# Layer 0's mixture of experts, from all experts inside the recurrence to picked experts behind it

## The chip, the cores and the metric

The kernel runs on one core of a Trainium2 chip. A core has five engines with their own instruction queues: PE (matrix products; its weight loads stand as PEld), DVE (vector), ACT (activation functions), POOL (general, here also the issuer of gathers and scatters) and SP (issues the plain transfers). [...] The metric is the time of one execution in microseconds (us), as the device reports it.

## What is computed

Four layers work on x (4 batches, 512 tokens, 256 numbers). Each adds an attention part and a feed-forward part, both behind a layer norm and a gate. Layer 0's attention part is an LSTM over the 512 tokens with an attention in each step, so its steps depend on each other. Its feed-forward part, which the change moves, is a mixture of 8 experts of which each token uses one:

```python
x = x + tanh(g_xattn[0]) * L0_xattn(ctx, layernorm(x), ...)        # LSTM, 512 steps
x = x + tanh(g_ffn[0])   * L0_ffn(layernorm(x), w1, b1, w2, b2, wr, br)

def L0_ffn(x, w1, b1, w2, b2, wr, br):            # x: 2048 tokens of 256
    probs = softmax(x @ wr + br)                  # 8 experts
    top_p, top_i = top_k(probs, 2)
    gate, top1 = top_p[:, 0] / (top_p[:, 0] + top_p[:, 1]), top_i[:, 0]
    for e in range(8):                            # w1[e]: 256 x 1024, w2[e]: 1024 x 256
        hout = gelu(x @ w1[e] + b1[e]) @ w2[e] + b2[e]
        out += where(top1 == e, hout * gate, 0)
```

Layer 1 has a cross attention of x with the context in both directions, and 8 gated experts of which two are used; layer 2 an additive attention and 8 experts with those kept that hold 0.8 of the probability; layer 3 a 16-head attention and a quantised product.

## The kernel before, in words

**Recurrence.** `lstm` loads the weights, and `recurrence` runs over 512 steps (`lstm_step`). A step is a chain that goes from engine to engine: products with the hidden state (PE), a transposition (DVE, L821), tanh (ACT, L832 and L837), scores (PE, L844), softmax (DVE and ACT, L855 to L864), products with the attention's weights (PE, L868), gates (DVE L877, ACT L880), cell and hidden state (L886 to L897). L897, on DVE, writes the new hidden state and ends the step.

Other work is put in the gaps of the steps by a planner, `Later`. It holds tasks in queues by engine and kind (`soon`, `chain`, `bulk`, `down`), with what they wait for and a cost, and `later.fill(engine, budget)` writes the next ready ones at fixed places of the step: on PE after the scores (`SLOT_B` tasks) and after the attention's products (`SLOT_C`), on ACT, DVE, POOL and SP at one place each. After the last step `later.drain()` writes all that is left.

After each 64 steps `block_tasks` adds the tasks of that block of 64 tokens by 4 batches (256 tokens): load x (L513), the cell's gates (L529, L541), cell and hidden state (L552 to L565), add to x (L590). Then come layer norm, router and, for each of the 8 experts on all 256 tokens, 32 instructions of products up (L720), gelu (L730), 32 down (L751) and the weighted sum into x (L758). Weights of 1 MB come through `net.fetch` into a ring of three places for `up` and three for `down` (L122, L125). At the end the block goes back into `xtok` (L799), which holds x for all tokens. ACT's Exp and Tanh share a function table, while gelu and Sqrt each need another: the step reloads its own at L895.

`net.fill` copies x into DRAM scratch, 2 MB at a time, once each 8 steps (L94), so that no unset row is read later.

**Tail.** Behind the recurrence layers 1 and 2 use picked experts alone. `picks_of` sorts one batch: layer norm, router (`ranked`), weights, the place of each pick (`g_to`), and indirect DMAs on POOL that scatter the rows by expert into DRAM (L1227). A group is two batches. `Blocks` computes a group in blocks of one expert: `load` reads the expert's number and its rows' place into registers on SP and loads rows and weights (L1293) into the same ring, `turn` transposes the rows, `work_1` or `work_2` does the products (L1392 to L1431 are its activations), `out` stores the result. `sure` computes the first `kind.sure` blocks, and `rest` enters a branch if the group has more (L1457), which computes `kind.step` blocks, all through one ring place. `back` gathers the results by indirect DMAs (L1481) and adds them to `xtok` (L1473, DVE).

PE's instructions keep the order in which the program writes them (`Ordered`), so `weave(main, side, ratio)` sets it: after each step of `main`, `ratio` steps of `side`. The order of the tail before: layer 1's context, attention of batch 0, attention of batch 1 together with batch 0's sort, batch 1's sort, then layer 1's first group beside batches 2 and 3, and so on through the layers. The products of all of the tail stand under the helper's line, L940.

Of the kernel before, what the change touches and what calls it, by code (L numbers as in the profile page):

```python
# [21 lines left out]
FP = mybir.dt.float32  # L22
# [7 lines left out]
P = 128  # L30
# [4 lines left out]
TPB = S // P  # L35
# [5 lines left out]
SLOT_B, SLOT_C = 2, 2  # L41
# [4 lines left out]
class Net:  # L46


    def __init__(self, ctx, tc, a):
# [26 lines left out]
        self.at = {"up": 0, "down": 0}  # L76
        self.ready = {part: deque() for part in ("up", "down")}
        self.coming = {part: deque() for part in ("up", "down")}
        for part in self.coming.values():
            part.extend((0, e) for _ in range(NBLK) for e in range(NE))  # L80
# [29 lines left out]

    def fetch(self, part=None):

        nc, a = self.nc, self.a
        for part in (part,) if part else ("up", "down"):
            if not self.coming[part]:
                continue
            layer, e = self.coming[part].popleft()
            i = self.at[part] % 3
            self.at[part] += 1
            if part == "down":  # L120
                w = self.ring[:, i, 1].rearrange("p (f d) -> p f d", d=D)
                nc.sync.dma_start(w, a[f"L{layer}_w2"][e])  # L122
            else:
                w = self.ring[:, i, 0].rearrange("p (k f) -> p k f", k=KD)
                nc.sync.dma_start(w, a[f"L{layer}_w1"][e])  # L125
            self.ready[part].append((layer, e, w))

    def take(self, part, layer, e):
        got = self.ready[part].popleft()
        assert got[:2] == (layer, e)  # L130
        return got[2]
# [113 lines left out]
def lstm(net):  # L245
    tc, nc, a = net.tc, net.nc, net.a
    with ExitStack() as st:
# [19 lines left out]
        with tc.tile_pool(name="l_set", bufs=1) as pool, tc.tile_pool(  # L267
# [22 lines left out]
            net.fetch()  # L290
            net.fetch()
# [64 lines left out]
            down=st.enter_context(tc.tile_pool(name="l_down", bufs=2, space=PSUM)),  # L356
        )
# [3 lines left out]
def recurrence(net, w, pools):  # L361
# [3 lines left out]
    moe0 = load_moe0(net, one)  # L365
# [18 lines left out]
    for t in range(S):  # L384
        i, u = divmod(t, P)
        if u == 0 and i + 1 < TPB:
            norm_x(net, later, w, pools, xb, i + 1)
        v = t % TB
        if v == 0:
            n = t // TB  # L390

            assert n < 3 or all(x["at"] for x in used[n - 3])
            hb = two.tile([P, 2, TB, NB], FP, name="hb", bufs=3)
            cb = two.tile([P, 2, TB, NB], FP, name="cb", bufs=3)
        if t % 32 == 0 and t and t // 32 + 1 < NJ:
            gates_of_block(net, later, w, pools, xb, ge, t // 32 + 1)
        lstm_step(net, pools["step"], ps, w, later, ge, t, h, hb[:, :, v], cb[:, :, v], ga[t % 2], ga[1 - t % 2])
        h = hb[:, :, v]
        if t > TB and t % 8 == 4:
            net.fill()  # L400
        if v == TB - 1:
            used.append(block_tasks(net, later, w, moe0, pools, n, hb, cb))
# [77 lines left out]
def load_moe0(net, pool):  # L480
    nc, a = net.nc, net.a
    m = {}
    m["wr"] = pool.tile([P, KD, NE], FP, name="m0_wr")
    nc.sync.dma_start(m["wr"], a["L0_wr"])
    m["br"] = pool.tile([P, NE], FP, name="m0_br")
    nc.sync.dma_start(m["br"], a["L0_br"].partition_broadcast(P))
    m["b1"] = pool.tile([P, NE, 8], FP, name="m0_b1")
    nc.sync.dma_start(m["b1"], a["L0_b1"])
    m["b2"] = pool.tile([NE, D], FP, name="m0_b2")
    nc.sync.dma_start(m["b2"], a["L0_b2"])  # L490
    return m


def block_tasks(net, later, w, m, pools, n, hb, cb):
# [5 lines left out]
    one, two, up, down = pools["one"], pools["two"], pools["up"], pools["down"]  # L500
    box = {}
    add = later.add

# [73 lines left out]
    sums = []  # L577
    for p in range(2):
# [16 lines left out]
        def total(p=p):  # L595
            if p == 0:
                box["st"] = two.tile([P, 2, 6], FP, name="st")
                box["mv"] = two.tile([P, 2, 2], FP, name="mv2")
            yield nc.vector.bn_stats(box["st"][:, p, :], box["xh"][:, p, :])
            yield nc.vector.bn_aggr(box["mv"][:, p, :], box["st"][:, p, :])  # L600

        t = chain("PE", turn, hs, takes=["up"], frees=[("g2", acts[0])] if p else [])
        chain("DVE", lambda put=put: put(0), [t, loaded], 0.5)
        p1 = chain("DVE", lambda put=put: put(1), [t, loaded], 0.5, frees=[("up", t)])
        sums.append(chain("DVE", total, [p1], 0.8))

    def root():
        box["rs"] = two.tile([P, 2], FP, name="rs")
        later.table = "sqrt"
        yield nc.scalar.activation(box["rs"], box["mv"][:, :, 1], AF.Sqrt, bias=net.eps)  # L610

    r = chain("ACT", root, sums)
    r = chain("DVE", lambda: [nc.vector.reciprocal(box["rs"], box["rs"])], [r], 0.2)
    outs = []
    for p in range(2):
        cell = {}

        def normal(p=p, cell=cell):
            cell["xn"] = two.tile([P, D], FP, name="xn")
            yield nc.gpsimd.tensor_scalar(  # L620
                cell["xn"], box["xh"][:, p, :], box["mv"][:, p, 0:1], box["rs"][:, p : p + 1],
                ALU.subtract, ALU.mult,
            )

        def turn(cell=cell):
            cell["ps"] = up.tile([P, KD, P], FP, name="ps_xt", tag="up")
            for k in range(KD):
                yield nc.tensor.transpose(cell["ps"][:, k, :], cell["xn"][:, ts(k, P)], net.ident)

        def out(p=p, cell=cell):  # L630
            if p == 0:
                box["x"] = two.tile([P, KD, 256], FP, name="xm")
            yield nc.scalar.copy(box["x"][:, :, ts(p, P)], cell["ps"])

        k = chain("POOL", normal, [r], takes=["xn"])
        t = chain("PE", turn, [k], takes=["up"], frees=[("xn", k)])
        outs.append(chain("ACT", out, [t], cost=0.6, frees=[("up", t)]))


    def logits():  # L640
        box["pr"] = up.tile([P, 2, NE], FP, name="ps_route", tag="up")
        for p in range(2):
            for k in range(KD):
                yield nc.tensor.matmul(
                    box["pr"][:, p, :], lhsT=box["x"][:, k, ts(p, P)], rhs=m["wr"][:, k, :],
                    start=k == 0, stop=k == KD - 1,
                )

    head = last = chain("PE", logits, outs, takes=["up"])

    def tile(name, *shape):
        box[name] = two.tile([P, *shape], FP, name=f"r_{name}")
        return box[name]

    v, N2 = nc.vector, (2, NE)
    steps = [
        lambda: v.tensor_add(tile("lg", *N2), box["pr"], bc(m["br"], 1, 2)),
        lambda: v.tensor_reduce(tile("mx", 2), box["lg"], AX.X, ALU.max),
        lambda: v.tensor_sub(tile("e", *N2), box["lg"], bc(box["mx"], 2, NE)),
        "exp",  # L660
        lambda: v.tensor_tensor(tile("over", *N2, NE), bc(box["e"], 2, NE), bc(box["e"], 3, NE), ALU.is_gt),
        lambda: v.tensor_tensor(tile("same", *N2, NE), bc(box["e"], 2, NE), bc(box["e"], 3, NE), ALU.is_equal),
        lambda: v.tensor_mul(box["same"], box["same"], bc(net.before, 1, 2)),
        lambda: v.tensor_add(box["over"], box["over"], box["same"]),
        lambda: v.tensor_reduce(tile("rank", *N2), box["over"], AX.X, ALU.add),
        lambda: v.scalar_tensor_tensor(tile("two", *N2), box["rank"], 1.5, box["e"], ALU.is_lt, ALU.mult),
        lambda: v.tensor_reduce(tile("den", 2), box["two"], AX.X, ALU.add),
        lambda: v.reciprocal(box["den"], box["den"]),
        lambda: v.scalar_tensor_tensor(box["two"], box["rank"], 0.5, box["e"], ALU.is_lt, ALU.mult),
        lambda: v.tensor_mul(tile("comb", *N2), box["two"], bc(box["den"], 2, NE)),  # L670
        lambda: v.tensor_scalar_mul(box["comb"], box["comb"], net.gate[:, 1, 0:1]),
    ]
    for i, f in enumerate(steps):
        if f == "exp":
            last = chain("ACT", lambda: [nc.scalar.activation(box["e"], box["e"], AF.Exp)], [last], 0.4)
        else:
            last = chain("DVE", lambda f=f: [f()], [last], 0.3, frees=[] if i else [("up", head)])


    def turn():  # L680
        box["pc"] = up.tile([NE, 2, P], FP, name="ps_ct", tag="up")
        for p in range(2):
            yield nc.tensor.transpose(box["pc"][:, p, :], box["comb"][:, p, :], net.ident)

    def out():
        box["cT"] = two.tile([NE, 256], FP, name="cT")
        yield nc.scalar.copy(box["cT"], box["pc"].rearrange("p b t -> p (b t)"))

    comb = last
    t = chain("PE", turn, [comb], takes=["up"])  # L690
# [1496 lines left out]
```

## Time and profile before

| what | value |
| --- | --- |
| median of 10 runs | 5555.59 us (5550.56 to 5563.15) |
| the profiled execution's own time | 5553.95 us |
| its span, first to last instruction | 5552.2 us |
| instructions | 142169 |
| PE, DVE, ACT, POOL busy | 86%, 44%, 48%, 8% of the span |
| first and last L897 (step ends) | 53.4 and 3379.0 us |
| first turn of layer 1's first block | 3823.4 us |
| four branches of `rest` | all not entered |

How to read it: an engine's busy time is the union of its instructions' times, and a product's own time includes its way through a pipeline, so that many of 0.4 us follow each other each 0.22 us. In a group's row, after the count, come busy time, the mean of one in ns, and the engine's idle time just before with what ended it. "DVEq" or "PEldq" is an engine's sequencer. A window's row gives its length, then the busy time of each engine that took part.

### The profile page before, as it was taken

The page shows a single profiled execution, that of the slowest core. Times are in us where ns is not written, and L with a number is a line of the kernel's source. Part 1 is how long each engine was busy: PE and PEld are TensorE (multiplying, and loading weights), DVE is VectorE, ACT ScalarE, POOL GpSimd, SP SyncE. Part 2 cuts the span into 40 slices and gives each one's busy share as a digit, 9 for nine tenths or more (in the row PEclk, how much of TensorE's full clock was granted, in tenths as well). Part 3 has the DMA queues.
Part 4 walks back from the last instruction along what each step waited for, and adds up shares of the span by engine and source line. Part 5 has one row for each costly group of instructions (what it writes and reads, how often), then busy time and mean ns, then how long its engine had stood idle before and what let it go on. Part 6 is the DMA issues. An engine that isn't in the chain of part 4 may idle for free. (4 is left out here: it accounts for less than half of the span.)

```text
span 5552.2 us, 142169 instructions
## 1 busy us (share of the span) xinstructions
PE 4760.0 (86%) x57504; PEld 2662.8 (48%) x57504; DVE 2443.1 (44%) x10804; ACT 2683.0 (48%) x8540; POOL 465.4 (8%) x884
## 2 busy tenths in 40 slices
PE   5667799999999999999999999987988599869967
PEld 2223344444444444444444446864533365757744
DVE  3555555555555555555555552123523332121145
ACT  2344565656665656566666663211266165213212
POOL 1000000100000100100000010001111201130030
PEclk8999999999999999999999999998999799989968
DMA  5000012112212112112212102413644333544210
GB/s 204 2 2 2 10 70 92 63 66 78 85 70 87 63 63 102 55 70 80 77 63 85 56 33 96 140 62 110 197 139 129 135 114 127 180 160 141 93 52 8
DMA packets 117988, 480.66 MB, mean 87 GB/s; under 512 B 23473, under 2 KB 62787, under 8 KB 87939
## 3 DMA queue, kind: packets, MB, share of 16 engines
q1 hardware_dynamic: 105026, 437.85, 22.4%
q0 software_dynamic: 12288, 33.57, 1.8%
q8 instruction: 455, 7.45, 0.6%
q14 instruction: 219, 1.79, 0.1%
HBM read 434.65 MB, written 137.89 MB: 103 GB/s over the span
## 5 line engine op out<-in xcount | busy, mean ns | idle before, releaser
L844 PE MATMUL psr<-e,vrep 128*32 128x64 f32 x16384 | 590.8, 232 | 50.0 <-ACT e L832 47.3
L868 PE MATMUL psf<-fw,alb 128*4 128x256 f32 x8192 | 540.6, 381 | 100.6 <-DVE alb L864 96.0
L844 PEld LDWEIGHTS psr<-e,vrep 128*32 128x32 f32 x16384 | 390.5, 108 | 409.9 <-ACT e L832 287.0
L720 PE MATMUL ps_up<-xm,ring 128*128 128x256 f32 x2048 | 546.9, 398 | 8.7 <-ACT h L730 8.3
L825 PE MATMUL psf<-whh,hb 128*4 128x256 f32 x8176 | 543.0, 383 | 0.7 <-issue 0.7
L751 PE MATMUL ps_down<-ring,h 128*128 128x256 f32 x2048 | 542.4, 396 | 0.0
L832 ACT ACTIVATE e<-fproj,hw 128x64 f32<-128x64 f32 x1024 | 297.9, 337 | 364.0 <-DVE hw L821 363.9
L880 ACT ACTIVATE ga<-gt 128x24 f32<-128x24 f32 (+1 forms) x1024 | 170.4, 214 | 572.5 <-DVE gt L877 571.3
L855 DVE TENSOR_REDUCE stat<-psr 128x1 f32<-128x64 f32 x1024 | 230.2, 225 | 448.5 <-PE psr L844 448.5
L720 PEld LDWEIGHTS ps_up<-xm,ring 128*128 128x128 f32 x2048 | 356.7, 189 | 143.2 <-issue 79.8
L751 PEld LDWEIGHTS ps_down<-ring,h 128*128 128x128 f32 x2048 | 359.1, 189 | 131.2 <-issue 83.3
L856 ACT ACTIVATE al<-psr,stat 128x64 f32<-128x64 f32 x1024 | 320.4, 313 | 183.0 <-DVE stat L855 183.0
L877 DVE STREAM_TRANSPOSE gt<-psf 128x192 f32<-128x192 f32 (+1 forms) x1024 | 263.1, 295 | 321.6 <-PE psf L868 321.1
L816 PE MATMUL psa<-wh,hb 128*4 128x64 f32 x8176 | 209.4, 220 | 203.4 <-DVE hb L897 199.3
L940 PE MATMUL ps_up<-xT,ring 128*128 128x256 f32 x1280 | 309.5, 393 | 72.2 <-ACT h L1429 48.8
L1721 ACT ACTIVATE h<-featT,txtT 128x512 f32<-128x512 f32 x512 | 324.7, 711 | 96.8 <-PE psr L940 62.2
L474 PE MATMUL psf<-ge,ident 128*4 128x256 f32 x4096 | 320.8, 385 | 57.4 <-DVE gt L877 57.3
L836 DVE TENSOR_TENSOR e<-fproj,hw 128x128 f32<-128x128 f32 x1536 | 361.5, 290 | 17.6
L898 POOL COPY cb<-ga 128x8 f32<-128x8 f32 x512 | 96.9, 189 | 3151.7 <-DVE ga L890 3151.7
L837 ACT ACTIVATE e<-e 128x128 f32<-128x128 f32 x1536 | 354.8, 293 | 2.6 <-DVE e L836 2.1
L816 PEld LDWEIGHTS psa<-wh,hb 128*4 128x4 f32 x8176 | 114.4, 86 | 463.5 <-DVE hb L897 463.5
L868 PEld LDWEIGHTS psf<-fw,alb 128*4 128x4 f32 x8192 | 123.1, 84 | 422.9 <-DVE alb L864 413.2
(418 smaller groups left out, 6438.3 us busy)
## 6 DMA issues: line engine op xcount, KB each, us to landing
ring<-in_L_w_dram SPq DMA_DIRECT2D x208, 1024.0 KB
ring<-in_L_w_dram SPq DMA_DIRECT2D x120, 512.0 KB
res<-y SPq DMA_DIRECT2D x120, 128.0 KB
rows_in<-rows SPq DMA_DIRECT2D x40, 256.0 KB
rows_in<-rows SPq DMA_DIRECT2D x40, 128.0 KB
rows<-in_x_dram SPq DMA_DIRECT2D x2, 1920.0 KB
res<-in_x_dram SPq DMA_DIRECT2D x2, 1920.0 KB
xtok<-in_x_dram SPq DMA_DIRECT2D x4, 512.0 KB
```

Of the source, the lines that this page charges most:

```text
L474: net.tc.keep_in_program_order(net.nc.tensor.matmul(out[32 * q : 32 * q + NB, :], lhsT=sel, rhs=ge[t // 32][:, ts(q, 256)], start=True, st ...
L720: yield nc.tensor.matmul(cell["ps"][:, f % 2, :], lhsT=ex["w"][:, k, ts(f, P)], rhs=box["x"][:, k, :], start=k == 0, stop=k == KD - 1,)
L751: yield nc.tensor.matmul(cell["ps"], lhsT=ex["h"][:, f, ts(p, P)], rhs=ex["down"][:, f, :], start=f == 0, stop=f == 7,)
L816: pin(nc.tensor.matmul(ps["a"][32 * q : 32 * q + NB, :], lhsT=h[:, c, :], rhs=w["wh"][:, c, ts(q, 64)], start=c == 0, stop=c == 1,))
L825: pin(nc.tensor.matmul(psf[32 * q : 32 * q + NB, :], lhsT=h[:, c, :], rhs=w["whh"][:, c, ts(q, 256)], start=False, stop=False,))
L836: pin(nc.vector.tensor_add(e[:, p, c], w["fproj"][:, p, c], bc(hw[:, c, ts(p, 2)], 2, SC)))
L837: pin(nc.scalar.activation(e[:, p, c], e[:, p, c], AF.Tanh))
L844: pin(nc.tensor.matmul(ps["r"][p][ts(2 * b + i, 32), :], lhsT=w["vrep"][:, c, :], rhs=ev[:, ::-1, :] if i else ev, start=c == 0, stop=c == ...
L856: pin(nc.scalar.activation(al[:, p], ps["r"][p], AF.Exp, bias=stat[:, p, 0:1], accum_out=stat[:, p, 1:2]))
L868: pin(nc.tensor.matmul(psf[32 * q : 32 * q + NB, :], lhsT=alb[:, p], rhs=w["fw"][:, p, ts(q, 256)], start=False, stop=p == 1,))
L940: return lambda *a, **k: self.tc.keep_in_program_order(fn(*a, **k))
L1721: nc.scalar.activation(h, featT[:, ec, :], AF.Tanh, bias=w["txtT"][:, ec, col : col + 1])
```

## The change

- `block_tasks` ends with the new x of the block, which goes straight to `xtok`. Norm, router, experts and their fetches leave the recurrence, `load_moe0`, `fetch` and `take` with them. `SLOT_B` goes from 2 to 1, and `net.fill` runs each 6 steps, since four more scratch tensors are to be filled.
- Layer 0 becomes a third `Kind`: one pick a token, blocks of 256, 8 sure blocks, 3 in `rest`. `top_1` makes its weights, `second_bias` (out of `top_p`) adds the second bias, `work_2` gets Gelu.
- The tail's order: both sorts of group 0 taken in turns with both contexts; group 0's blocks beside group 1's sorts, `rest`; group 1's blocks beside the gathers of group 0, layer 1's attention of batches 0 and 1 and their sorts, `rest`; then layer 1's first group, with the gathers of group 1 ahead of its side work.

```diff
-SLOT_B, SLOT_C = 2, 2
+SLOT_B, SLOT_C = 1, 2
...
-        if t > TB and t % 8 == 4:
+        if t > TB and t % 6 == 4:
             net.fill()
         if v == TB - 1:
-            used.append(block_tasks(net, later, w, moe0, pools, n, hb, cb))
+            used.append(block_tasks(net, later, w, pools, n, hb, cb))
...
         t = chain("PE", turn, hs, takes=["up"], frees=[("g2", acts[0])] if p else [])
         chain("DVE", lambda put=put: put(0), [t, loaded], 0.5)
-        p1 = chain("DVE", lambda put=put: put(1), [t, loaded], 0.5, frees=[("up", t)])
-        sums.append(chain("DVE", total, [p1], 0.8))
-    def root():
...
+        done = chain("DVE", lambda put=put: put(1), [t, loaded], 0.5, frees=[("up", t)])
...
-    add("SP", store, [last_put], frees=[("block", loaded)])
+    chain("SP", store, [done], frees=[("block", loaded)])
...
-KINDS = {1: Kind(1, 2, 128, 20, 3), 2: Kind(2, 6, 256, 20, 4)}
+KINDS = {0: Kind(0, 1, 256, 8, 3), 1: Kind(1, 2, 128, 20, 3), 2: Kind(2, 6, 256, 20, 4)}
...
+def top_1(t, pool, m, b, rank, key, keep, comb):
+
+    v, net = t.nc.vector, t.net
+    v.scalar_tensor_tensor(comb, rank, 1.5, key, ALU.is_lt, ALU.mult)
+    den = pool.tile([P, TPB], FP, name="g_den")
+    v.tensor_reduce(den, comb, AX.X, ALU.add)
+    v.reciprocal(den, den)
+    v.tensor_scalar_mul(den, den, net.gate[:, 1, 0:1])
+    v.tensor_single_scalar(keep, rank, 0.5, ALU.is_lt)
+    v.tensor_mul(comb, keep, key)
+    v.tensor_mul(comb, comb, bc(den, 2, NE))
+    yield
+    yield from second_bias(t, pool, m, b, comb)
...
-                    if i >= self.on_scalar:
+                    if self.kind.layer == 0:
+                        nc.scalar.activation(h[:, f, :], ps[:, n, :], AF.Gelu, bias=bias)
+                    elif i >= self.on_scalar:
...
-            context_l1(t, w1, p1)
-            pk = Picks(t, sort)
...
-            b1 = Blocks(t, KINDS[1], first, got[1][1], KINDS[1].sure % 3)
-            b0 = Blocks(t, KINDS[1], first, got[1][0], 0, b1)
-            run(behind(1, l1, 0))
-            weave(b0.sure(), chain(behind(1, l1, 2), context_l2(t, w2, p2)), 1.1)
+            def contexts():
+                for _ in range(2):
+                    yield
+                context_l1(t, w1, p1)
+                yield
+                yield from context_l2(t, w2, p2)
...
+            with tc.tile_pool(name="sort_too", bufs=1) as too:
+                run(turns(sorted_by(0, 0), sorted_by(0, 1, {"sort": too}), contexts()))
+            yg = work_1.enter_context(tc.tile_pool(name="first_back", bufs=1))
+
+            def back_0(g):
+                return back(t, yg, KINDS[0], groups[g], groups[g], got[0][g], 4)
+
+            with tc.tile_pool(name="zero", bufs=2) as zero:
+                b0 = Blocks(t, KINDS[1], None, got[1][0], at[2])
+                a1 = Blocks(t, KINDS[0], zero, got[0][1], at[1], b0)
+                a0 = Blocks(t, KINDS[0], zero, got[0][0], at[0], a1)
+                weave(a0.sure(), chain(sorted_by(0, 2), sorted_by(0, 3)), 0.8)
+                a0.rest()
+                weave(a1.sure(), chain(back_0(0), behind(1, l1, 0)), 1.6)
+                a1.rest()
+            first = beside("first", 2)
+            b0.pool, b0.next = first, Blocks(t, KINDS[1], first, got[1][1], at[3])
+            b1 = b0.next
+            weave(b0.sure(), chain(back_0(1), behind(1, l1, 2)), 1.1)
             b0.rest()
```

## The prediction, on record before the changed kernel ran

> **What bounds the kernel now.** I read the page's busy table first (PE 86%), then the step times of the recurrence, then the stretches behind it, then who waits there, because the share of 86% is a mean over stages with different limits. Layer 0's mixture stands on the page as its two products:
>
> ```profile
> L720 PE MATMUL ps_up<-xm,ring 128*128 128x256 f32 x2048 | 546.9, 398 | 8.7 <-ACT h L730 8.3
> L751 PE MATMUL ps_down<-ring,h 128*128 128x256 f32 x2048 | 542.4, 396 | 0.0
> ```
>
> The means overlap: in a dense stretch 32 of them take 7.07 us, 0.22 us each, so the 4096 need some 905 us of PE. What they cost in time is less, since most lie in gaps of the recurrence. The rows of L897 (one a step), counted in two windows: columns are window, length, busy time (times), clock, DMA share, GB/s.
>
> ```profile
> 100.00:500.00 400.00, 10.66 (x64) 0.99 0.01 2
> 800.00:3200.00 2400.00, 68.14 (x370) 1.00 0.20 74
> ```
>
> Without the mixture a step takes 400/64 = 6.25 us, with it 2400/370 = 6.49. So the recurrence is bound by its own chain of small dependent steps, and the mixture adds 0.24 us a step. The rest of its price comes when the recurrence ends, at 3379. Stretches from there (length, then busy PE, PEld, DVE, ACT, POOL, clock, DMA share, GB/s):
>
> ```profile
> 3379.00:3682.00 303.00, 291.85 (x1336) 249.43 (x1334) 29.75 (x85) 78.23 (x180) 11.20 (x10) 1.00 0.36 125
> 3682.00:3703.00 21.00, 11.56 (x36) 7.44 (x36) 5.58 (x16) 0.00 (x0) 0.00 (x0) 0.76 0.34 113
> 3703.00:3741.00 38.00, 32.22 (x110) 16.82 (x110) 13.32 (x28) 10.42 (x15) 0.00 (x0) 0.94 0.00 0
> 3741.00:3793.00 52.00, 41.85 (x136) 23.74 (x136) 26.08 (x83) 11.82 (x19) 8.22 (x8) 0.80 0.06 21
> 3793.00:3823.00 30.00, 6.93 (x28) 5.96 (x28) 13.98 (x72) 2.69 (x5) 7.75 (x8) 0.50 0.12 40
> 3823.00:4035.00 212.00, 193.32 (x730) 114.66 (x730) 94.73 (x248) 48.93 (x79) 15.48 (x16) 0.99 0.60 197
> ```
>
> 303 us of left-over mixture with PE full; 21 us of layer 1's context; layer 1's attention of batch 0 (38) and of batch 1 with batch 0's sort (52); batch 1's sort alone (30, PE idle for 23); then layer 1's first 20 blocks, PE full again. I compare both kernels at one point: the first turn of those blocks, at 3823.4 now. Behind it the code is nearly the same.
>
> **The change, stage by stage.**
>
> *Recurrence.* All of L720, L751, the router and their SP loads go. The three first steps end at 94.5 us (5.9, 26.5 and 8.7 long); 508 steps at 6.25 end at 3270. What stays of each block (gates, cell, hidden state) cost little before: in the first such stretch the long steps are those with a Sqrt, router steps or gelus, all removed. I allow 2 us a block, 14. End at **3285** (bounds 3262, by the commonest step of 6.23, and 3379, no gain). At nothing: the 72 scratch fills instead of 52, one each 6 steps (74 places), cover the recurrence's DMA, 20% busy, from which 128 MB of weights go. If they did delay anything, it would be x's loads for a block, due 64 steps later. The slot at B of 1 instead of 2: chain tasks number some 40 in 64 steps, and three fit a step.
>
> *Left-over work.* Only the last block's own chain: 7.1 us of L529, the six POOL steps and two more to 17 us behind their start (rows 3460.8 to 3477.7), minus 1.5 for a wait on a gelu, transposes and sums 2, stores landing 2: **19** us, to 3304.
>
> *Two sorts with both contexts.* The sort alone needs 16.6 us from its first statistics (3792.7) to the places (3809.3). The second sort shares PE and DVE with it (+8); context_l1 stands in PE's written order ahead of the second half of the turns (13.8 us, rows 3688.6 to 3702.3, and some 4 us more until its weights land); context_l2 adds 2. That is 45. Then batch 1's four scatters, and what comes behind the last of them, as now:
>
> ```profile
> 3818.57 0.97 POOL L1227 DMA_INDIRECT rows<-g_xs,g_to  x1 [0.30 <-issue]
> 3821.26 0.37 SPq L1293 DMA_DIRECT2D rows_in<-rows  x1
> 3823.43 0.66 PE L940 MATMUL ps_side<-ident,rows_in 128*128 128x128 f32 x2 [16.57 <-DMA rows_in<-rows]
> 3825.88 5.07 PE L940 MATMUL ps_up<-ring,xT 128*128 128x512 f32 x8 [1.79 <-DMA ring<-in_L_w_dram]
> ```
>
> 3 x 1.28 + 4.9 = 9: **54** (45 to 65), to 3358.
>
> *First group, 8 blocks.* A block of 256 with 1024 hidden units exists already, in layer 2; where nothing lies beside it:
>
> ```profile
> 4804.53 0.60 PE L940 MATMUL ps_side<-ident,rows_in 128*128 128x128 f32 x4
> 4804.97 7.07 PE L940 MATMUL ps_down<-ring,h 128*128 128x256 f32 x32
> 4811.87 7.07 PE L940 MATMUL ps_up<-xT,ring 128*128 128x256 f32 x32
> 4818.78 0.60 PE L940 MATMUL ps_side<-ident,rows_in 128*128 128x128 f32 x4
> ```
>
> 14.25 us, 114 for eight; first weights 2.5 (row 3825.9); the other two sorts' PE work 15 (router 3.6, the rest 4 each). ACT has one gelu of 0.42 us for each 0.9 us of PE, but each Sqrt or Exp between gelus means two table loads of 1.283 us: four such places, 10 us, of which 0 to 10 reach PE; I take 8, since the side's next product stands in PE's order and waits. **140** (131 to 150), to 3498.
>
> *What is over 8 blocks.* By the reference's router the picks of the two groups are 134, 60, 301, 70, 277, 29, 28, 125 and 139, 56, 292, 67, 299, 28, 23, 120: ten blocks each, two experts over 256. So `rest` is entered in both groups and computes three blocks (8 to 10, the last empty). No run of `rest` is in this trace: its four conditions were false. Even so a false one costs:
>
> ```profile
> 4033.00 0.42 DVE L1366 COPY y<-ps_down 128x256 f32<-128x256 f32 x1 [1.30 <-PE ps_down L940]
> 4034.69 0.41 PE L940 MATMUL ps_side<-ident,rows_in 128*128 128x128 f32 x2 [1.73 <-DVEq L1457]
> 4037.01 0.35 SPq L1293 DMA_DIRECT2D res<-y  x1
> ```
>
> PE's products ended at 4031.3: 3.3 us until PE goes on, 6 until SP does (its branch at 4037.4). Entered, SP reads two registers (1.4), loads rows (2.5) and weights (2 more): 12 until PE runs. Then 3 x 14.3 = 43, if one ring place is enough: the next `up` (1 MB, usable 3.7 us behind its issue, rows 3822.2 to 3825.9) is asked for as soon as this one's up is done and lands beside the 7 us of down, and the next down likewise. Exit 3.3. **58** (46, nothing but PE and exit; 75, each load waited for in the open), to 3556.
>
> [...]
>
> *Second group beside layer 1's attention of batches 0 and 1.* 114 of blocks and 32.2 + 41.9 + 6.9 = 81 us of PE work that stood bare before, in 120 us. That is where the change gains. Twelve Sqrt, Exp and Tanh places between gelus are 31 us of table loads; PE feels 0 to 31, I take 17. Eight gathers of `back`, on POOL at 1.26 us, hold DVE's queue for 14 us, about one block's products: 3. **215** (198 to 235), to 3771. POOL and SP are otherwise idle enough: SP issues some 6 transfers a block.
>
> *Its rest, and layer 1's first rows.* Layer 1's sort ends at step 82 of the side, main step 51, behind the last places (41 to 50) where its blocks could be loaded ahead. So instead of the exit of 3.3 it waits for SP (6), registers and rows (4): **65** (52 to 80), to **3836**, 13 us later than now.
>
> *Behind it.* context_l2 is gone from there (9 us: 7 of PE and the 1.8 that PE waits for it); eight more gathers ahead of layer 1's third batch cost DVE's order some 9. Zero.
>
> Sum: 5552.2 + 13 = 5565 of span, 1.75 us around it as in the profiled run (5553.95), 1.6 from that to the median shown (5555.59): **5569 us**, 0.24% slower. A measurement of this kernel tells about 0.2% from no change.
>
> **Rivals.**
>
> 1. *The weaves hide all.* If table loads and gathers cost PE nothing in the two groups (8 + 17 + 3) and the contexts fill the two sorts' gaps (-8), 36 go: 5533, faster. For it: the stretch 3823 to 4035 does 193 us of PE in 212 beside sorts and attention. Against: no gelu was there. It decides if PE's waits in both groups stay under some 10 us together.
>
> 2. *The gathers stall PE as they do now in two places:*
>
> ```profile
> PE ps_up L940 <- DVE xtok L1473: 16.6, 1, 16.6
> PE ps_up L940 <- ACT h L1429: 38.4, 1, 38.4
> ```
>
> At layer 1's second group (16 gathers) and layer 2's second (48). At two new places, 17 each instead of 3 and 9: +22; at 38 each +64. Nearest by count is the first: 5595 to 5633. Against: only 8 gathers, and gelu is on ACT, not DVE.
>
> 3. *One ring place is not enough*, and each block of `rest` waits for its loads: 3 x 6 a group, +34: 5603.
>
> 4. *`rest` is not entered* (counts differ on the chip): two times 55 less, 5459. The counts are 21 or more away from 256.
>
> **How the numbers follow.** Forecast, 5548 to 5592 by itself: 0.42. Rival 1: 0.27, rival 2: 0.15, rival 3: 0.13, rival 4: 0.03. Within 0.2% (5544 to 5567) lie 0.15 of the forecast and 0.04 of rival 1: 0.19. Faster: 0.23 + 0.03 = 0.26. Slower: 0.27 + 0.15 + 0.13 = 0.55. All lower ends of the stages give 5508, all upper ends 5640; with rivals 2 and 3 in and the ends of both sides out, 5520 to 5635.
>
> **What would show it.** Steps of 6.2 to 6.3 us throughout and an end near 3285; first turn of layer 0's blocks near 3358; eight turns 17 us apart; then 3 turns 14 to 15 us apart behind a gap of 12 (right), or 20 apart (rival 3); the second group at 27 us a block; layer 1's first turn near 3836. Wrong, if the recurrence keeps long steps, if a wait of over 15 us stands at either group's first gathers, or if PE is full through both groups.

## The result, and the profile after

The changed kernel takes 5594.18 us (median of 8 runs, 5581.72 to 5605.05) against 5555.52 us for the kernel before (28 runs): **0.68% slower**, a ratio of 1.0068 with a 95% interval of 1.0059 to 1.0076. The forecast was 5569, 25 us too low, on the right side of no change and inside the range of 5520 to 5635, though 2 us above the range of the forecast by itself (5548 to 5592). The profiled execution took 5605.77 us with a span of 5604.1, some 12 above its median; so the two profiled spans lie 51.9 us apart and the medians 38.7. Stages are compared by the spans.

The step rows first, L651 now, in the two windows in which the prediction counted L897 (length, DVE busy with the count, clock, DMA share, GB/s):

```profile
100.00:500.00 400.00, 10.71 (x64) 1.00 0.01 2
800.00:3200.00 2400.00, 70.67 (x377) 0.98 0.15 49
```

The second window holds 377 steps where 370 stood: 6.37 us a step, not the 6.25 of the first window that the prediction took for all. Then the stages behind the recurrence (length, then busy PE, PEld, DVE, ACT, POOL, clock, DMA share, GB/s): the last block's own chain with the first two sorts, group 0's woven blocks, its conditional run, group 1's woven blocks, its conditional run, layer 1's first group.

```profile
3331.70:3416.10 84.40, 48.93 (x168) 35.80 (x168) 32.77 (x149) 10.47 (x22) 16.91 (x16) 0.61 0.16 48
3416.10:3546.60 130.50, 128.41 (x624) 110.68 (x624) 29.57 (x102) 35.72 (x75) 7.76 (x8) 0.98 0.58 202
3546.60:3599.60 53.00, 45.66 (x206) 39.30 (x206) 4.62 (x9) 10.07 (x24) 0.00 (x0) 0.94 0.43 149
3599.60:3798.40 198.80, 186.69 (x817) 140.58 (x815) 68.78 (x209) 62.16 (x112) 23.27 (x24) 0.97 0.29 99
3798.40:3855.80 57.40, 46.17 (x205) 39.35 (x205) 5.05 (x10) 10.08 (x24) 0.44 (x1) 0.91 0.42 143
3855.80:4093.40 237.60, 199.35 (x713) 114.74 (x713) 99.36 (x265) 49.17 (x80) 24.34 (x26) 0.92 0.55 173
```

In the two woven groups PE is busy for 128 of 130 and 187 of 199 us: they are full. The time is lost in the first row (PE idle for 35 us, and at a clock of 0.61 where it works) and in the last (idle for 38).

| stage, us of the span | before | predicted | measured |
| --- | --- | --- | --- |
| fourth step ends | 94.5 | 94.5 | 103.3 |
| last step ends | 3379.0 | 3285 | 3331.7 |
| left-over work, two sorts, contexts | | 73 | 84.4 |
| group 0, 8 blocks | | 140 | 130.5 |
| its conditional run | | 58 | 53.0 |
| group 1, 8 blocks | | 215 | 198.8 |
| its conditional run, layer 1's first rows | | 65 | 57.4 |
| first turn of layer 1's blocks | 3823.4 | 3836 | 3855.8 |
| from there to group 1 of layer 1 | 211.3 | 211 | 237.6 |
| from there to the end | 1517.5 | 1517 | 1510.7 |

The misses against the forecast are +47 (recurrence, 9 of it before the fourth step), +11, -9.5, -5, -16, -8, then +26 and -7: 39 of span. What was lost against the forecast lies in three places: the recurrence, which gives back 47 us and not 94; the two sorts; and layer 1's first group. **Start.** DVE's longest waits between 45 and 100 us, after and then before:

```profile
DVE off L1473 <- DMA l_mask<-in_mask_dram: 44.4, 1, 44.4
```

```profile
DVE wslide L1676 <- DMA l_vec<-in_L_vec_dram: 20.2, 1, 20.2
```

Both are instructions of layer 2's context, put early into DVE's queue by the scheduler, and their loads stand in SP's queue behind scratch fills and the first blocks' rows. In before the second step waits (26.5 us long); after, the first step cannot start (it ends at 84.1, not 53.4).

**Steps.** 76 of the 508 steps behind the fourth take over 6.35 us. Together they are 62.6 us above 6.23 each, where I had allowed 24. 22 of them run beside POOL's work on the second cell's state. Here is a plain step and then such a step (start, duration, DVE instruction), and below it POOL's rows:

```profile
541.93 0.69 DVE L590 TENSOR_TENSOR e<-fproj,hw 128x128 f32<-128x128 f32 x3
544.70 0.22 DVE L618 SCALAR_TENSOR_TENSOR alb<-alT,stat,own 128x4 f32<-128x4 f32 x1
```

```profile
548.51 1.50 DVE L590 TENSOR_TENSOR e<-fproj,hw 128x128 f32<-128x128 f32 x3
550.94 0.20 DVE L616 STREAM_TRANSPOSE alT<-al 128x32 f32<-128x32 f32 x1
552.13 1.15 DVE L618 SCALAR_TENSOR_TENSOR alb<-alT,stat,own 128x4 f32<-128x4 f32 x1
```

```profile
550.64 1.26 POOL L508 TENSOR_TENSOR g<-g,cb 128x512 f32<-128x512 f32 x1
551.99 1.27 POOL L509 TENSOR_TENSOR g<-g 128x512 f32<-128x512 f32 x1
```

L618 works on four elements a partition and takes 0.22 us; beside POOL's 1.27 us operation it ends when POOL's does (both near 553.3 us). L616, beside POOL's operation of 1.26 us, keeps its 0.20. Both of the step's L618 (0.71 and 1.15 us) and the three instructions of L590 add up to 2.2 us more than in a plain step, and the step is 2.1 us longer (8.34 against 6.23).

The other 54 long steps (37.5 us) have no POOL work. Three hold a stop of PE with nothing to wait for (6.8 us), 33 run in part at a granted clock of 0.50 (24.9 us), and 18 are at 1.00 throughout (5.8 us). Of the 33, 15 come within three steps of POOL's work or of a stop, the others do not. Over the recurrence the clock's record holds 0.50 for 157 us in 32 pieces; in the kernel before it holds 34 us in 7 pieces. That the mixture's products had kept the clock up by filling PE's gaps is an inference from this; no run tests it.

### The profile page after: what moved, and what is told of

Same layout as the page of the kernel before. It is cut to its first block, busy times and chain, and to the rows that moved or that the text cites. A ratio compares the mean times of both kernels' runs of the same rounds, so it can differ in the third digit from the quotient of the medians.

```text
span 5604.1 us, 137309 instructions
## 1 busy us (share of the span) xinstructions
PE 4153.2 (74%) x54920; PEld 2240.2 (40%) x54920; DVE 2440.2 (44%) x10794; ACT 2079.1 (37%) x7635; POOL 479.7 (9%) x900
## 5 line engine op out<-in xcount | busy, mean ns | idle before, releaser
L579 PE MATMUL psf<-whh,hb 128*4 128x256 f32 x8176 | 564.8, 396 | 0.0
L694 PE MATMUL ps_up<-xT,ring 128*128 128x256 f32 x1984 | 474.5, 391 | 68.6 <-ACT h L1208 32.8
L694 PE MATMUL ps_down<-ring,h 128*128 128x256 f32 x1984 | 458.1, 387 | 16.2 <-ACT h L1206 8.1
L694 PEld LDWEIGHTS ps_up<-xT,ring 128*128 128x128 f32 x1984 | 379.3, 195 | 173.0 <-issue 58.9
L694 PEld LDWEIGHTS ps_down<-ring,h 128*128 128x128 f32 x1984 | 378.5, 194 | 91.5 <-issue 33.5
L590 DVE TENSOR_TENSOR e<-fproj,hw 128x128 f32<-128x128 f32 x1536 | 361.7, 290 | 17.6
L443 PEld LDWEIGHTS psf<-ge,ident 128*4 128x4 f32 x4096 | 61.5, 89 | 521.9 <-DVE gt L631 509.2
```

The lines of the kernel that those rows point to most:

```text
L443: net.tc.keep_in_program_order(net.nc.tensor.matmul(out[32 * q : 32 * q + NB, :], lhsT=sel, rhs=ge[t // 32][:, ts(q, 256)], start=True, st ...
L579: pin(nc.tensor.matmul(psf[32 * q : 32 * q + NB, :], lhsT=h[:, c, :], rhs=w["whh"][:, c, ts(q, 256)], start=False, stop=False,))
L590: pin(nc.vector.tensor_add(e[:, p, c], w["fproj"][:, p, c], bc(hw[:, c, ts(p, 2)], 2, SC)))
L694: return lambda *a, **k: self.tc.keep_in_program_order(fn(*a, **k))
```

## The experiments

My theory was: the change loses by what its conditional runs cut (preloads on both sides), by a sort that ends too late in layer 1's first group, by the mask's wait, and by POOL's work in the recurrence, which the mixture had nothing to do with. The rivals are named with each run. The first four ran on one chip, the next four on a second, the last three on a third; the kernel before took 5554.13, 5473.62 and 5557.14 us there, so runs of different chips are compared by ratio and by stage. On the second chip everything from layer 1's second group on takes 1435 to 1437 us in either kernel, on the others 1504 to 1518; the stages before it agree with the other chips.

**Ten woven blocks.**

```diff
-KINDS = {0: Kind(0, 1, 256, 8, 3),
+KINDS = {0: Kind(0, 1, 256, 10, 3),
```

> Ten of layer 0's blocks a group in the woven run instead of eight, so that neither conditional run is entered. Theory (a conditional run loses the preloads on both its sides): in the changed kernel the two stretches from the end of the eighth block to the next group's first turn took 59.8 and 65.1 us; two more blocks inside the woven run cost 2 x 15.4 us (123.6 / 8, the pace of group 0's woven blocks) each time and the next group's rows are there at once, so 29 + 34 = 63 us less: about 5531 us. Rival (the conditional run costs what its blocks cost, and only its empty third block is waste): a block less in each group, 2 x 12 to 15 us, about 5567 us.

Measured: 5532.9 us, ratio 0.9955 (0.9942 to 0.9968), 61 less than the changed kernel: the theory's number. From group 0's first turn to group 1's 160.6 us instead of 183.4, from there to layer 1's first turn 226.6 instead of 256.3. (The expectation put the end of the eighth block 7 us too early, before its last product; the sums are the same.) PE's first rows behind group 0's woven blocks: as changed, where the conditional run starts, then here, where group 1 starts:

```profile
3551.91 1.09 PE L694 MATMUL ps_side<-ident,rows_in 128*128 128x128 f32 x4 [5.28 <-DMA rows_in<-rows]
3554.58 9.06 PE L694 MATMUL ps_up<-xT,ring 128*128 128x256 f32 x32 [1.58 <-DMA ring<-in_L_w_dram]
```

```profile
3571.34 0.63 PE L694 MATMUL ps_side<-ident,rows_in 128*128 128x128 f32 x4 [0.30 <-PEq L1236]
```

With the run entered PE waits 5.28 us for rows and 1.58 for weights, and then a block's products take 9.06 instead of 7.07 us. Skipped, it waits 0.30 us ahead of the next group's turn.

**Two blocks in the conditional run.** `Kind(0, 1, 256, 8, 2)`.

> The conditional run takes two blocks instead of three, so the empty block goes and the conditional run stays. Theory (lost preloads): the first two turns and the late first rows of the next group stay; only the third turn's 12 to 15 us go, in part covered by the next loads, 10 to 25 us less in all: 5570 to 5584 us, at least 30 us above the run without conditional runs. Rival (only the empty block is waste): the same time as the run without conditional runs, within 10 us, about 5567 us.

Measured: 5563.41 us, ratio 1.0017 (1.0007 to 1.0026), 31 less than the changed kernel and 30.5 above the run before. So half of the price is the empty block (11.7 and 12.8 us in the two groups), half the lost preloads. The gain is 6 above the theory's upper end: layer 1's first group is 7 us shorter too, which I can't assign.

**More side pieces in layer 1's first group.**

```diff
-            weave(b0.sure(), chain(back_0(1), behind(1, l1, 2)), 1.1)
+            weave(b0.sure(), chain(back_0(1), behind(1, l1, 2)), 1.4)
```

> Layer 1's first group with 1.4 side pieces a turn instead of 1.1. Theory (the gathers put ahead of the attention make the last sort end at 4075.8, after the group's last turn, so that group 1's first rows can't be preloaded and PE stands idle 10.7 us): the gap from 4082.7 to 4093.4 closes to under 3 us and the tail of the stage shortens, 8 to 18 us less: 5576 to 5586 us. Rival (the stage is longer by its gathers' adds on DVE and by the lower clock, 0.91 against 1.00): no change, 5590 to 5597 us.

Measured: 5579.13 us, ratio 1.0049 (1.0037 to 1.0061), 15 less. PE's row at the end of the stage, changed and here:

```profile
4093.37 0.66 PE L694 MATMUL ps_side<-ident,rows_in 128*128 128x128 f32 x2 [10.71 <-DMA rows_in<-rows]
```

```profile
4060.97 0.41 PE L694 MATMUL ps_side<-ident,rows_in 128*128 128x128 f32 x2 [1.36 <-DVEq L1236]
```

The wait of 10.71 us for rows is 1.36: the theory of its cause holds. What this is worth is not shown. The stage took 226.3 us instead of 237.6, but in five runs without this edit (the two before, the next, and the two behind that) it took 226.8 to 234 us with the wait for rows in place (9.0 to 10.8 us). In the stage behind, PE now waits 15.13 us for a sum of gathered rows (DVE L1252) where the changed kernel waited 5.01. And the recurrence was 18 us shorter in this profiled run, with no change to it.

**Mask early.**

```diff
+        self.mask = keep.tile([P, NB * SC], I32, name="l2_mask")
+        nc.sync.dma_start(self.mask, a["mask"].partition_broadcast(P))
...
-    nc.sync.dma_start(w["mask"], a["mask"].partition_broadcast(P))
+    w["mask"] = net.mask
```

> Layer 2's mask is loaded ahead of the recurrence's weights, not behind 8 MB of scratch fills. Theory (DVE's queue waits for it from 49.6 to 77 us, ahead of the first step): the first step ends near 57 instead of 84.1 us and the fourth near 76 instead of 103.3, 27 us less: 5567 us. Rival (the first steps wait for their own weights and rows as well, in the same crowded queues): under 8 us less, 5586 to 5594 us.

Measured: 5558.69 us, ratio 1.0009 (0.9999 to 1.0018), 35 less. The first step ends at 54.4 and the fourth at 72.8 us, 30 earlier. The theory holds.

**Cell state on DVE, one operation a step.**

```diff
-    hs = chain("POOL", cell_state, acts)
+    hs = None
+    for k in range(6):
+        hs = chain("DVE", lambda k=k: cell_state(k), [*acts, hs])
...
-    hs = [chain("POOL", lambda c=c: hid(c), [hs]) for c in range(2)]
+    hs = [chain("DVE", lambda c=c: hid(c), [hs]) for c in range(2)]
```

> The second cell's state of each block of 64 steps (six operations and two products, 128x512 and 128x256) is computed by DVE, one operation a step, in the place after the softmax where DVE waits for PE (about 1 us a step), and no longer by POOL in one burst of 7.3 us. Theory (POOL's operations slow DVE's short ones that run beside them, 0.22 to 0.71 and 1.15 us, and the long step is followed by steps at a lower clock): the 22 steps with POOL's burst (25 us above 6.23 in all) and some 8 us of the steps behind them come back: about 30 us less, 5564 us. Rival (the long steps are the block's own matmuls and loads, and eight more DVE instructions a block in the step cost what they take, 64 x 0.5 us): no gain or up to 30 us more, 5594 to 5625 us.

Measured: 5481.86 us, ratio 1.0012 (1.0003 to 1.0021), 0.0056 below the changed kernel's, or 31 us. The step rows in the second of the two windows:

```profile
800.00:3200.00 2400.00, 63.62 (x381) 0.99 0.15 49
```

381 steps in place of 377. The steps with POOL work lose 24.7 of their 25.0 us above 6.23, and L618 is never longer than 0.4 us, where it was 14 times of 1024. DVE's eight operations of 0.42 to 0.69 us cost nothing: one stands between L618 and the next transposition, where DVE waits for PE anyway. The rival is refuted. The other long steps have 27.6 us in place of 37.5; that is no proof of an effect on them, since they have 22.6 to 36 in runs that leave POOL's work as it was.

**Fills on POOL.**

```diff
-            self.tc.keep_in_program_order(self.nc.sync.dma_start(x, self.a["x"][0 : x.shape[0], :]))
+            self.tc.keep_in_program_order(self.nc.gpsimd.dma_start(x, self.a["x"][0 : x.shape[0], :]))
```

> The scratch fills (72 transfers of 2 MB) are issued by POOL, at the same steps, and no longer from SP's queue, where they wait behind the stores of the recurrence's blocks and then go out up to nine at a time. Theory (a bunch of fills keeps the DMA engines full, PE's matmuls then stop with nothing to wait for, 1.4 us each time, and the granted clock falls to 0.5 to 0.67 for two or three steps behind it): the steps without POOL work above 6.35 us lose 15 to 20 of their 37 us: 5574 to 5579 us. Rival (the stops have another cause, or POOL's own work at a fill slows DVE as its other work does, 72 x 0.5 us): no gain, or up to 36 us more, 5594 to 5630 us.

Measured: 5468.31 us, ratio 0.999 (0.9981 to 0.9999), 0.0078 or 43 us less. 30 of these were not foreseen by either theory: with the fills out of SP's queue the mask lands in time (first step at 54.7 us). The steps without POOL work fall from 37.5 to 21.3 us above 6.23, as the theory says, and PE's unexplained stops (three of 1.4 us in the changed kernel) are gone. But the run with more side pieces had 22.6 us and one stop (1.85 us), with the fills on SP. So this run alone settles nothing on the stops.

**The kernel before, mask early.**

> The kernel before, with layer 2's mask loaded ahead of the recurrence's weights. Theory (the stall at the start is one that both kernels have; the change only moved it from the second step to ahead of the first and made it 9 us longer): the second step of 26.5 us becomes one of 6.3 to 7, about 20 us less: 5535 us. Rival (it comes with the change, by the fills that start earlier): under 5 us less, 5550 to 5556 us.

Measured: 5474.13 us, ratio 1.0004 (0.9995 to 1.0013). Both numbers missed, in favour of neither: the second step still waited, 19.6 us for `l_vec`. I had taken the mask for the culprit, but DVE's row names another load (above: `wslide <- l_vec`). The kernel before had the same sort of stall at another instruction.

**The four repairs together.**

> Ten woven blocks, 1.4 side pieces a turn, the mask early and the cell state on DVE together. If the theories hold and the parts do not touch each other: the run with ten woven blocks at 5533 us, less 35 (mask), less 30 (cell state), less some 8 (weave, whose stage was 11 us shorter in that run already): about 5460 us. If the cell state on DVE gives nothing (its rival): about 5490 us or more.

Measured: 5384.6 us, ratio 0.9846 (0.9831 to 0.9861). The forecast of 5460 was for the first chip and amounts to 0.983, at the lower end of the interval. The four gains measured alone are 0.0247 of the kernel before together, here 0.0222: the parts add up, nearly.

**The kernel before, mended likewise.** Mask and vector table early, cell state on DVE.

> The kernel before with the same two repairs as far as they fit it: layer 2's mask and vector table are loaded ahead of the recurrence's weights, and the second cell's state of each block is computed by DVE, one operation a step. Theory (before's second step of 26.5 us is DVE's queue waiting 20.2 us for the vector table, put ahead by the same scheduler; its 33 steps with POOL work cost 26.6 us above 6.23): the fourth step ends near 75 instead of 94.5 us, the steps with POOL work lose some 25 us, about 45 us less than the kernel before on the same chip, a ratio of 0.992. Rival (the eight DVE operations a block have no free place in a step that also carries the mixture's work): the start's 20 us alone, 0.996, or no gain.

Measured: 5516.52 us, ratio 0.9927 (0.9914 to 0.9941). The fourth step ends at 73.8 us, and the steps with POOL work have 3.0 us above 6.23 instead of 26.6. The theory's number; the last step ends 40 us earlier, 21 of it by the start.

**All repairs and fills on POOL.**

> The changed kernel with ten woven blocks, 1.4 side pieces, early mask, the cell state on DVE, and the scratch fills issued by POOL. Theory (bunched fills stop PE and lower the clock): the steps above 6.35 us without POOL work lose 10 to 15 of the 25.5 us that they have in the run with the fills on SP: ratio 0.982. Rival (that share varies from run to run, 22.6 to 37.5 us in runs with the fills on SP): the ratio of that run within its interval, 0.983 to 0.986, and two more stops in PE or none, as it falls.

Measured: 5453.95 us, ratio 0.9811 (0.9797 to 0.9824), under the rival's interval. The steps without POOL work have 14.3 us above 6.23, and PE has no stop in the recurrence. Over all profiled runs of the changed code: with the fills on SP 22.6 to 37.5 us and 1 to 5 stops of over 1.1 us in each of seven; with them on POOL 12.7 to 21.3 us and no stop in three. This speaks for the theory, not with certainty: the kernel before also has its fills on SP, and no such stop in its three profiles. What PE lacks in a stop is not shown.

**Contexts beside group 0.**

```diff
-                run(turns(sorted_by(0, 0), sorted_by(0, 1, {"sort": too}), contexts()))
+                run(turns(sorted_by(0, 0), sorted_by(0, 1, {"sort": too})))
...
-                weave(a0.sure(), chain(sorted_by(0, 2), sorted_by(0, 3)), 0.8)
+                weave(a0.sure(), chain(sorted_by(0, 2), sorted_by(0, 3), contexts()), 0.8)
```

> As the run before it, with the contexts of layers 1 and 2 woven beside layer 0's first group, behind the sorts, and no longer between the first two sorts. Theory (the 84 us from the last step to the first block's turn are a chain through all engines in which PE's order puts the contexts, 14.6 us, ahead of the router's product, while PE has holes beside the blocks): 10 to 15 us less ahead of the first turn, at most 5 more in the blocks, 8 to 12 us less in all, ratio 0.002 lower. Rival (PE is full beside the blocks, 15.4 us a block): what goes ahead of the first turn comes back in the first group, no change.

Measured: 5453.64 us, ratio 0.9812 (0.9798 to 0.9825), no change. From the last step to the first block's turn 64.8 us instead of 76.9, as the theory says; group 0's ten blocks 170.5 instead of 161.2, as the rival says. PE was busy for 159 of those 161 us: work moved beside it comes back.

## Why the prediction was right or wrong

- **Side and size.** Slower was right. But 5594.18 lies 2 us above the forecast's own range and 1 us below rival 2's (5595 to 5633), and two of the three signs that the prediction named for being wrong came: long steps in the recurrence, and PE all but full in both groups. The stages missed by some 129 us in all, and 39 were left because they missed to both sides: that the sum came so near is in part luck. That it lost more than 0.24% comes from two terms that were set too low and one that was set at zero.
- **Recurrence, 3285: the failed step.** "In the first such stretch the long steps are those with a Sqrt, router steps or gelus, all removed" was a wrong reading. The steps of 8.3 to 8.8 us carry POOL's burst, which stays: moving it off POOL takes away 25 us of the 62.6. Of the mixture itself the profile of before holds 92.4 us of long steps without POOL work, and 37.5 of such stay. I had seen which instructions stood in a long step, not which of them had become longer. A second term was put at nothing without being named: the granted clock, 0.99 and 1.00 in the rows of before, which I took to stay there without the mixture. The 33 steps that run in part at a clock of 0.50 lose 24.9 us, where before lost 5.2 in 7 such steps.
- **The first steps, +9.** Taken over unchanged from before; the wait moved to another instruction and grew. The early mask gives 30 us back, in a place that the prediction left out since it was not part of the change.
- **Two sorts, 19 + 54, measured 84.4.** The last block's chain was right: the first statistics start 18.6 us behind the last step's end. The sorts took 65.8 us. I had read the 16.6 us of a sort from layer 1, which has no second bias; in layer 0's sorts PE computes that bias, in its written order, ahead of the products that give the places. Layer 1's sort of before, then layer 0's two:

```profile
3805.83 0.60 PE L940 MATMUL ps_side<-g_keep,upper 128*128 128x32 f32 x2 [2.96 <-DVE g_keep L1156]
```

```profile
3388.30 0.17 DVE L933 TENSOR_SCALAR g_keep<-g_rank 128x32 f32<-128x32 f32 x1
3391.02 7.19 PE L694 MATMUL ps_side<-m_b,combT 8*128 8x256 f32 x16
3398.14 0.64 PE L694 MATMUL ps_side<-g_keep,upper 128*128 128x32 f32 x2
```

So the places come some 9 us later. And both sorts' places come together, at 3401 and 3402, so that eight scatters and not four stand between them and the first turn: 14.3 us instead of 9. Of the 20 us that the sum gave to the contexts, taking them out gave 12 in the last run. No run moved the second bias.
- **The two groups, 140 and 215, measured 130.5 and 198.8.** Of my charges of 8, 17 and 3 us for table loads and gathers one wait of 8.1 us for a gelu came (3610 to 3618 us), and its source is the gathers, charged 3, not the table loads, charged 25:

```profile
3609.51 0.48 DVE L1252 SCALAR_TENSOR_TENSOR xtok<-yg,g_cw,xtok 128x256 f32<-128x256 f32 x1 [8.62 <-DMA yg<-res,g_index]
3616.29 0.30 ACT L739 ACTIVATE ln_rstd<-ln_mv,eps 128x4 f32<-128x4 f32 x1 [9.42 <-DVE ln_mv L737]
3618.43 3.78 PE L694 MATMUL ps_down<-ring,h 128*128 128x256 f32 x8 [8.12 <-ACT h L1206]
```

DVE stands at the first gathered row, ACT at the Sqrt behind DVE's sums, the gelus behind that Sqrt, and PE at the gelu. PE was idle for 14 us in both groups, close to rival 1's point of decision of 10. So rival 1 was nearly right about the groups; its gain went under in the recurrence and in the last term below.
- **The conditional runs, 58 and 65, measured 53.0 and 57.4.** Mechanism and size were right, rival 3 (a ring place too few) was wrong: the third turn waited 0.49 us. The ten blocks came from the reference's counts, so rival 4 fell. What I did not draw from it is what the run with ten woven blocks shows: of the 110 us, 52 can be had back in these stages.
- **"Behind it: zero", measured +26.** I wrote that eight more gathers cost DVE's order about what context_l2 had cost. The removal of context_l2 had another effect: it had stood at the end of the side work, so that the last sort ended ahead of the group's last blocks. Now the sort is last and the next group's rows come late (10.7 us). The gathers were not covered either: DVE stands 8.57 us at their first row, and PE waits 6.06 and, at 3874, 6.24 us for what stands behind it in DVE's queue:

```profile
3861.22 0.48 DVE L1252 SCALAR_TENSOR_TENSOR xtok<-yg,g_cw,xtok 128x256 f32<-128x256 f32 x1 [8.57 <-DMA yg<-res,g_index]
3862.54 5.24 PE L694 MATMUL ps_up<-ring,xT 128*128 128x512 f32 x8 [6.06 <-DVE ln_stats L736]
```

In all PE was idle for 38.3 us of this stage, where it had been for 18.3; the other 6 of the 26 are PE's own busy time, at a clock of 0.92 in place of 0.99. Rival 2's one wait of 16.6 us did not come, but its mechanism did, in shorter waits: 8.1 us in group 1 and 12.3 here, 20 in all, where I had charged 3 and 9.
- **Where the expected gain went.** With repairs on both sides the changed code takes 5453.95 us and the mended kernel before 5516.52, 1.1% apart; the repairs are not the same list, since conditional runs, weave and fills on POOL concern the changed code or were tried there alone. Ten woven blocks alone bring the change to 0.9955, faster than before; the 61 us that they are worth is about all of the 63 us by which the two mended kernels differ. So picked experts behind the recurrence pay, but hardly with 8 sure blocks where 10 are needed.

## What to carry to other kernels

Work that rides in the gaps of a latency-bound loop costs less than its engine time: of the mixture's 4096 products 2823 ran inside the recurrence, some 620 us by the 0.22 us of each, and 47 us came back. A conditional tail costs more than its blocks: here about half of its price was an empty block and half the preloads that it cuts on both sides, so the unconditional count should cover the common case. The side work of a weave should end before the last place from which the next group is loaded. Work read from a like stage must be compared line by line: a sort with one product more was priced as one without. When a loop has long steps, compare each instruction's own duration with that of a plain step before naming a culprit.

## What the runs showed of the hardware

In the step above with POOL's work some of DVE's instructions take longer than in the plain step, and others do not. The two instructions of L618 take 0.71 and 1.15 us in place of 0.22 and end when POOL's operations end (551.93 and 553.28 us beside 551.90 and 553.26), while the transposition keeps its 0.20. Of the three instructions in L590's row of 1.50 us two take 0.68 and 0.69 us and the third 0.28, as in the plain step, with POOL at work beside all three. What tells the one sort from the other is not shown.

PE's granted clock falls 32 times in the changed kernel's recurrence, and no gap of PE in the 20 us ahead of any of these falls is longer than 1.41 us. In the traces of both kernels the clock's record holds two values alone, 1.00 and 0.50; anything between in a row is a mean. The windows around a stop of 1.39 us, which ends at 1466.6 us in the changed kernel, and around one of 1.85 us, which ends at 1094.7 us in the run with more side pieces (columns as in the table of stages):

```profile
1462.69:1466.10 3.41, 1.74 (x39) 0.65 (x33) 1.28 (x6) 1.40 (x6) 0.19 (x1) 1.00 1.07 351
1466.10:1483.16 17.06, 13.07 (x207) 5.54 (x207) 6.74 (x35) 5.01 (x24) 0.38 (x2) 0.50 0.55 176
```

```profile
1087.00:1094.74 7.74, 5.14 (x111) 2.31 (x111) 3.85 (x21) 2.48 (x12) 0.19 (x1) 1.00 0.97 301
1094.74:1111.00 16.26, 12.27 (x259) 5.36 (x263) 7.67 (x40) 6.56 (x29) 0.57 (x3) 1.00 0.06 21
```

In the first case the clock is at 0.50 for 17 us; the step with the stop takes 8.88 us and the two behind it 7.83 and 6.99, in place of 6.23, so that this stop of 1.4 us costs 5. The two other stops of the changed kernel cost 2.9 and 2.8. In the second case the clock stays at 1.00, and a longer stop costs 1.7. Which gaps do it is open, since the stop of 1.85 us was followed by no fall in the 16 us shown.
